# Six row products for four rows in the first convolution, the projection behind the gate, and input statistics on ScalarE

## The chip, the cores and the metric

The kernel runs on one core of a Trainium2 chip. The metric is the device time of one execution in microseconds (us). The three timed runs of the kernel before gave 3256.61, 3258.98 and 3260.0 us; their median is 3258.98 us.

## The reference, cut to what matters

The input `x` is float32 with shape 4 x 64 x 256 x 256. Two residual layers follow each other, each fed through a group norm (32 groups of two channels).

```python
# layer 0: x = x + L0(gn(x))
h = gelu(conv3x3(x, c1_w) + c1_b)               # 64 -> 64 channels
xa, k = split(c1x1(h, c2_w, c2_b))              # 64 -> 64 + 64
xs = gelu(depthwise 3x1 (depthwise 1x3 (xa)))
mask = top 2 of softmax(mean(xs over the image) @ gate_w.T)
out = xs + sum_i mask[i] * c1x1(c1x1(k, w2_i) * c1x1(xs, w1_i), w3_i)   # ranks 2, 4, 8
return c1x1(out, proj_w, proj_b)

# layer 1: x = x + L1(gn(x))
h = relu(batchnorm(conv3x3(x, quantized w1)))
h = batchnorm(conv3x3(h, quantized w2))
return relu(h + x)
```

The gate needs the mean of `xs` over a whole image, so the experts' share of an image can be added only after its last row has passed.

## The kernel before

Activations stand with 64 channels in each half of the 128 partitions, so that four matmuls of 64 x 64 can run side by side in the array. The work has four stages in time: statistics of image 0 and the weights; the *front* (layer 0, image after image, and within it what of layer 0's output can already be finished); *conv1* (the first convolution of layer 1, with the rest of layer 0's output between its steps); *conv2*; and the end, which adds and stores.

The front goes in steps of 8 rows ("octs", 128 of them). For the first convolution it uses a scheme that makes two neighbouring pixels of a row from four products: GpSimd forms the four combinations of the input (`front_v`, L493 to L501, eight additions of 128 x 256 per oct, into a ring `v_ring`), TensorE multiplies them with four sets of weights for each of three row taps (`front_conv_a`, `front_conv_b`, L547 to L562, all through the matmul of L458), ScalarE copies a part (L567), VectorE adds and subtracts in place (`front_butterfly`, L568 and L569), the other two products are added on top, and ScalarE applies the GELU (`front_h`, L575). The vertical taps are matmuls into bank `a` (`front_taps_a`, `front_taps_b`), the horizontal taps two VectorE operations (`front_taps_h`), then a GELU that also sums for the gate (`front_xs`, L645). `front_k` and `front_q` make the experts' 14 ranks for four octs at a time. `front_proj` (L665 to L696) multiplies `xs` with the projection, VectorE adds it to the resident input, and the sum goes to memory (`t1_d`). After the gate, `out_slot` (L770 to L798) loads that sum back, adds the experts with a 32-row matmul, and keeps statistics of the result.

The statistics of the next image's input are VectorE `bn_stats` (`stats_group`, L403). Between two halves of the vertical taps stands a small GpSimd memset, `divide` (L449 to L453), which waits for the first half and releases the second.

The order of the work is written out by hand: `at(step, order, call)` puts a call into a table, and the table is emitted in sorted order, so every engine runs its instructions in the order of those two numbers. In the front this holds for TensorE, SyncE's DMA queue, VectorE and GpSimd; ScalarE's order there was left to the scheduler. Each oct has its own tile of PSUM for the convolution:

```python
BANKS = {"c": 2, "a": 1, "p": 1}
return psum.tile([P, 2, GP, W], F32, tag=tag, name=name, bufs=BANKS[tag])
...
at(g, 1, front_conv_a, b, n, (1, 2))
at(place(g + 1), 3, front_conv_a, b, n, (0, 3))
at(g, 7, front_conv_b, b, n, (1, 2))
at(g, 7.5, front_butterfly, b, n)
```

Of the kernel before, what the change touches and what calls it, by code (L numbers as in the profile page):

```python
# [9 lines left out]
F32 = mybir.dt.float32  # L10
# [8 lines left out]
P = 128  # L19

NPAIR = H // 2
NSKEW = NPAIR + 1
PW = W + 2
GP = 2
# [14 lines left out]

@with_exitstack
def conv_preact_kernel(ctx: ExitStack, tc: tile.TileContext, io, col128, colset, col64):
    nc = tc.nc

    x_s = io["x"].rearrange("b c (two r) w -> b (c two) (r w)", two=2)
    out_v = io["out"].rearrange("b c (r two) w -> b two c r w", two=2)
# [8 lines left out]
    BANKS = {"c": 2, "a": 1, "p": 1}  # L77

    def bank(tag, name):
        return psum.tile([P, 2, GP, W], F32, tag=tag, name=name, bufs=BANKS[tag])  # L80
# [5 lines left out]


    t1_d = [dram.tile([P, NPAIR, W], F32, name=f"t1_d{b}") for b in range(B)]

    low_d = [dram.tile([P, NOCT // 4, 2 * GF], F32, name=f"low_d{b}") for b in range(B)]  # L90
    y_d = [dram.tile([P, NPAIR, W], F32, name=f"y_d{b}") for b in range(B)]
    y_v = [t.rearrange("(par c) (q half) w -> half par c q w", par=2, half=2) for t in y_d]
# [5 lines left out]

    RING = max(CPAIR * PW, (CPAIR + 1) * W)

    def place_in(name, fourth=False):
        return (spare if fourth else ring).tile([P, RING], F32, tag="in", name=name)

    def chunk_in(name, fourth):

        t = place_in(name, fourth)
        return t[:, 0 : CPAIR * PW].rearrange("p (a b) -> p a b", b=PW)

# [34 lines left out]

# [9 lines left out]

# [3 lines left out]

    VSLOTS = 12
    v_rings = [front_pool.tile([P, VSLOTS, 2, W // 2], F32, name=f"v_ring{i}") for i in range(2)]

    def v_of(p):

        return v_rings[p in (0, 3)][:, :, p // 2, :]

# [6 lines left out]

# [4 lines left out]
    ones = const.tile([P, P], F32, name="ones")  # L176
    nc.vector.memset(ones, 1.0)
# [13 lines left out]
    outer = lconst.tile([P, 2, W], F32, name="outer")  # L191
    wk = lconst.tile([P, 2, 2, 32], F32, name="wk")
# [7 lines left out]

    def weights():
# [3 lines left out]
        m64 = flat(m64_t)[0:C, 0 : io["m64"].shape[1]]  # L205
        nc.sync.dma_start(mset, io["mset"])
        nc.sync.dma_start(m64, io["m64"])
# [8 lines left out]

        nc.vector.tensor_tensor(flat(av), cset("c2_a"), cset("sv"), ALU.mult)


# [14 lines left out]


# [4 lines left out]
        for s in range(2):  # L240
            half = slice(s * C, s * C + C)
            for i in range(2):
                o = 16 * (i ^ s)
                nc.vector.tensor_copy(wk[half, s, i, o : o + NLOW], ps[half, 0:NLOW])
        nc.vector.memset(both, 0.0)
# [9 lines left out]

# [21 lines left out]

    def combine(mv, n, avg, eps_t, out, name):

# [26 lines left out]

# [71 lines left out]
    gn1, gn2, c1s, u12, v_edge, c1_bias = {}, {}, {}, {}, {}, {}  # L383
# [3 lines left out]

    st_x, x_in = {}, {}
# [15 lines left out]

    def stats_end(b):


        own = stat.tile([P, 2], F32, tag="gx", name=f"gx_{b}")
        yield from group_norm(st_x.pop(b), c128("avgx"), own, f"x{b}")
        yield  # L410
        gn1[b] = stat.tile([P, 2], F32, tag="gn1", name=f"gn1_{b}")
        v_edge[b] = lstat.tile([P, W // 2], F32, tag="v_edge", name=f"v_edge_{b}")
        ps = small(f"ps_gx_{b}")
        nc.tensor.matmul(ps[:, 0:2], c128("from_x"), own, start=True, stop=True)
        nc.vector.tensor_copy(gn1[b], ps[:, 0:2])
        c1s[b] = lstat.tile([P, 3, 3, C], F32, tag="c1s", name=f"c1s_{b}")

        engine = nc.gpsimd if b else nc.vector
        engine.tensor_scalar(
            c1s[b].rearrange("p a b c -> p (a b c)"), c128("c1"), gn1[b][:, 1:2], None, ALU.mult  # L420
        )
        engine.tensor_scalar(v_edge[b], zeros[:, 0 : W // 2], gn1[b][:, 0:1], 2.0, ALU.add, ALU.mult)
        u12[b] = lstat.tile([P, 3, 2, C], F32, tag="u12", name=f"u12_{b}")
        ends = lstat.tile([P, 3, C], F32, tag="u_ends", name=f"u_ends_{b}", bufs=1)
        engine.tensor_tensor(ends, c1s[b][:, :, 0, :], c1s[b][:, :, 2, :], ALU.add)
        for i, op in enumerate((ALU.add, ALU.subtract)):
            engine.tensor_tensor(u12[b][:, :, i, :], ends, c1s[b][:, :, 1, :], op)
        u = u12[b].rearrange("p a b c -> p (a b c)")
        engine.tensor_scalar(u, u, 0.5, None, ALU.mult)  # L429

        engine.tensor_tensor(ends[:, 0, :], u12[b][:, 0, 0, :], u12[b][:, 1, 0, :], ALU.add)
        for half in (slice(0, C), slice(C, P)):
            engine.tensor_tensor(both[half, half], ends[half, 0, :], u12[b][half, 2, 0, :], ALU.add)
        yield
        ps = small(f"ps_cb_{b}")
        nc.tensor.matmul(ps[:, 0:1], both, gn1[b][:, 0:1], start=True, stop=True)
        c1_bias[b] = stat.tile([P, 1], F32, tag="c1b", name=f"c1b_{b}")
        nc.vector.scalar_tensor_tensor(c1_bias[b], ps[:, 0:1], -2.0, c128("c1_b"), ALU.mult, ALU.add)


    xs_of, hs, xss, k_sb, pooled, open_c, open_a, open_t, open_p = {}, {}, {}, {}, {}, {}, {}, {}, {}


# [25 lines left out]
    def front_alloc(b, k):  # L469
        c = b * NCH + k  # L470
        if c % 5 == 3:
            xs_of[b, k] = chunk_x(f"x_{b}_{k}")
        else:
            xs_of[b, k] = chunk_in(f"x_{b}_{k}", c % 5 == 4)

    def front_load(b, k):

        x = xs_of[b, k]
        for half, slot, first in ((0, 0, 0), (0, 1, 1), (1, 0, 3), (1, 1, 2)):
            row = 2 * k * CPAIR + first  # L480
            nc.sync.dma_start(
                x[half * C : half * C + C, slot::2, 1 : 1 + W],
                io["x"][b][:, row : row + 4 * CG - 3 : 4, :],
            )

    def front_pad(b, k):
        edges = zeros[:, 0 : 2 * CPAIR].rearrange("p (a b) -> p a b", b=2)
        nc.gpsimd.tensor_scalar(xs_of[b, k][:, :, 0 : PW : PW - 1], edges, gn1[b][:, 0:1], None, ALU.add)

    def v_slot(b, n, slot):  # L490
        return (4 * (b * NOCT + n) + slot) % VSLOTS

    def front_v(b, n, half, products=((1, 2), (0, 3))):  # L493

        x = xs_of[b, n // 2]
        i = 4 * (n % 2) + 2 * half
        d = [x[:, i : i + 2, q : q + W - 1 : 2] for q in range(4)]
        terms = {0: (d[0], d[2], ALU.subtract), 1: (d[1], d[2], ALU.add), 2: (d[2], d[1], ALU.subtract), 3: (d[3], d[1], ALU.subtract)}
        o = v_slot(b, n, 2 * half)
        for p in (p for ps in products for p in ps):  # L500
            nc.gpsimd.tensor_tensor(v_of(p)[:, o : o + 2, :], *terms[p])  # L501

    def conv_tile(b, n, t, in_half, products, first, last):


        ps = open_c[b, n][:, t].rearrange("p a b -> p (a b)").rearrange("p (e q c) -> p e q c", e=2, q=GP)
        terms = {
            (0, 0): ([(1, 0), (2, 1)], [(0, 0), (1, 1)]),
            (0, 1): ([(0, -2)], [(2, 1)]),
            (1, 0): ([(0, 1)], [(2, 2)]),  # L510
            (1, 1): ([(1, 1), (2, 0)], [(0, 1), (1, 0)]),
        }[t, in_half]

        def pieces(slot, p):
# [822 lines left out]
```

## Time and profile before

| what | value |
|---|---|
| median of three runs | 3258.98 us |
| span of the profiled execution, first to last instruction | 3255.8 us |
| instructions | 61027 |
| TensorE (PE) busy | 2664.0 us, 82% |
| VectorE (DVE) busy | 2665.1 us, 82% |
| ScalarE (ACT) busy | 1647.6 us, 51% |
| GpSimd (POOL) busy | 1603.1 us, 49% |
| DMA moved | 832.01 MB, mean 256 GB/s |
| mean granted TensorE clock | 0.924 |

The runs' median is 3.2 us above the span of the profiled execution, whose own time outside its span the page does not give. The chain that ended last is 40% TensorE, 10% waits in SyncE's queue (in the end stage), 8% VectorE. A line of a group reads: source line, engine, operation, output <- input, shape, number of instructions, busy time and mean nanoseconds of one, then the idle time of the engine before them and what ended most of it. One float32 `matmul` of the program shows as two instructions. The clock is given as a share of full speed.

### The profile page before, as it was taken

The numbers are of one execution on the slowest core, as the hardware profiler recorded it, in microseconds if no ns is written. First come the engines' busy times: TensorE is split into PE (matmuls) and PEld (weight loads), VectorE is DVE, ScalarE is ACT, GpSimd is POOL, SyncE is SP. The second block draws the span as 40 slices with busy tenths as digits, with TensorE's granted clock in tenths as the row PEclk, the third lists the DMA queues.
The fourth block names the chain that finished last, engine by engine and source line by source line (L and its number), as shares of the span: only waits on it lengthen the run. The fifth ranks groups of instructions, "written<-read, shape, count | busy, mean of one in ns | idle before, by whom it ended". The sixth has DMA issues, their size and how long they took to land.

```text
span 3255.8 us, 61027 instructions
## 1 busy us (share of the span) xinstructions
PE 2664.0 (82%) x25080; PEld 1756.5 (54%) x25080; DVE 2665.1 (82%) x2810; ACT 1647.6 (51%) x1799; POOL 1603.1 (49%) x1833
## 2 busy tenths in 40 slices
PE   2999999999999999999999999989999999300000
PEld 1555555555555555555676677768787878200000
DVE  7676588878888777777899999979999999876655
ACT  0444443444434344446666666767777777432222
POOL 2444544444444534445687787757777777100000
PEclk9999999999999999999999999999999999655555
DMA  8665689879987777766788886656666663799999
GB/s 306 175 182 131 161 270 287 246 212 289 277 272 219 217 203 210 214 195 207 283 288 298 292 315 220 245 194 229 238 234 233 245 223 124 261 412 412 413 412 377
DMA packets 355591, 832.01 MB, mean 256 GB/s; under 512 B 22192, under 2 KB 284848, under 8 KB 293360
## 3 DMA queue, kind: packets, MB, share of 16 engines
q1 hardware_dynamic: 355312, 828.11, 76.5%
q8 instruction: 197, 3.23, 0.4%
q14 instruction: 82, 0.67, 0.1%
HBM read 489.85 MB, written 338.17 MB: 254 GB/s over the span
## 4 chain that ended last, share of the span: by engine, by line
PE 40%; SPq 10%; DVE 8%; DMA 3%; issue 3%; ACT 2%; POOL 1%; ACTq 0%; DVEq 0%; POOLq 0%
PE ps_h L316 22%; SPq L1224 7%; PE ps_c L458 5%; PE ps_h2m L316 4%; PE ps_a L458 3%; SPq L1219 2%; PE ps_hm L316 2%; DVE half L362 2%; DMA yn<-y_d 2%; DVE h L342 2%; PE ps_o L778 1%; PE ps_p L458 1%; SPq L1203 1%; DVE st_h L874 1%; DMA y_end<-y_d 1%
## 5 line engine op out<-in xcount | busy, mean ns | idle before, releaser
L316 PE MATMUL ps_h<-half,w_q 128*128 128x512 f32 x4096 | 1026.4, 402 | 20.4 <-DVE h L342 13.7
L316 PEld LDWEIGHTS ps_h<-half,w_q 128*128 128x128 f32 x4096 | 772.7, 190 | 249.4 <-DVE h L342 24.0
L381 POOL TENSOR_TENSOR sum<-s,sum 128x640 fp32r<-128x640 f32 (+1 forms) x256 | 557.2, 2197 | 199.4 <-ACT sum L379 193.8
L501 POOL TENSOR_TENSOR v_ring<-x 128x256 f32<-128x256 f32 x1024 | 591.2, 613 | 48.4 <-DMA x<-in_x 46.5
L458 PE MATMUL ps_c<-v_ring,u 64*64 64x256 f32 (+1 forms) x6472 | 389.1, 369 | 4.7 <-DVE u L429 3.5
L458 PE MATMUL ps_a<-h,av 64*64 64x512 f32 (+1 forms) x3568 | 383.5, 533 | 11.0 <-DVE t L628 8.6
L458 PE MATMUL ps_c<-v_ring,c1s 64*64 64x256 f32 (+1 forms) x6472 | 386.6, 370 | 5.0 <-POOL tick L451 4.5
L342 DVE SCALAR_TENSOR_TENSOR h<-ps_h,scale_w,m 128x1024 f32<-128x1024 f32 x256 | 326.7, 1276 | 73.0 <-ACT m L341 72.9
L575 ACT ACTIVATE h<-ps_c,c1b 128x512 f32<-128x512 f32 x256 | 174.1, 742 | 403.5 <-PE ps_c L458 403.5
L458 PEld LDWEIGHTS ps_c<-v_ring,c1s 64*64 64x64 f32 x6472 | 250.5, 133 | 202.3 <-issue 72.2
L458 PEld LDWEIGHTS ps_c<-v_ring,u 64*64 64x64 f32 x6472 | 270.4, 133 | 144.0 <-POOL v_ring L501 66.0
L451 POOL MEMSET tick<- 128x1 f32 x132 | 13.0, 98 | 679.2 <-PE ps_a L458 668.5
L645 ACT ACTIVATE xs<-t 128x1024 f32<-128x1024 f32 x128 | 135.4, 1058 | 368.9 <-DVE t L631 351.4
L1215 ACT ACTIVATE v<-y_end,shift,gn 128x2048 f32<-128x2048 f32 x64 | 133.8, 2092 | 293.8 <-DMA y_end<-y_d 260.9
L362 DVE TENSOR_TENSOR half<-h,half 128x1280 fp32r<-128x1280 f32 (+1 forms) x128 | 254.3, 2028 | 7.7 <-ACT half L360 7.7
L1216 DVE SCALAR_TENSOR_TENSOR h<-h,ss,v 128x2048 f32<-128x2048 f32 x64 | 149.9, 2349 | 134.5 <-ACT v L1215 84.4
L690 DVE TENSOR_TENSOR x<-ps_p,x 128x1024 f32<-128x1024 f32 x128 | 156.1, 1219 | 101.1 <-PE ps_p L458 69.0
L568 DVE TENSOR_TENSOR ps_c<-m,ps_c 128x512 f32<-128x512 f32 x128 | 89.0, 695 | 175.8 <-ACT m L567 175.7
L458 PEld LDWEIGHTS ps_a<-h,av 64*64 64x64 f32 x3568 | 163.5, 133 | 128.5 <-issue 91.7
L362 DVE TENSOR_TENSOR half<-yn,half 128x1280 fp32r<-128x1280 f32 x80 | 202.7, 2551 | 0.0
L341 ACT ACTIVATE m<-ps_hm,m,scale_w 128x512 f32<-128x512 f32 x128 | 99.4, 777 | 183.2 <-PE ps_hm L316 153.9
L786 DVE SCALAR_TENSOR_TENSOR y<-ps_o,ob,y 128x1024 f32<-128x1024 f32 x128 | 163.6, 1278 | 15.1 <-PE ps_o L778 10.9
(186 smaller groups left out, 4083.5 us busy)
## 6 DMA issues: line engine op xcount, KB each, us to landing
h_d<-h SPq DMA_DIRECT2D x114, 1024.0 KB, 4.8
h<-h_d SPq DMA_DIRECT2D x64, 1152.0 KB, 7.1
yn<-y_d SPq DMA_DIRECT2D x60, 1152.0 KB, 8.3
xs_in<-in_x SPq DMA_DIRECT2D x64, 1024.0 KB, 9.0
x<-in_x SPq DMA_DIRECT2D x256, 256.0 KB, 5.3
y<-t_d SPq DMA_DIRECT2D x64, 1024.0 KB, 8.8
y_d<-y SPq DMA_DIRECT2D x256, 256.0 KB, 5.1
y_end<-y_d SPq DMA_DIRECT2D x64, 1024.0 KB, 10.8
```

The costliest lines, as they stand in the source:

```text
L316: nc.tensor.matmul(ps[:, 0 : n * HW], w[:, k, m, :], t[:, i + m : i + m + n, c : c + HW], start=(j == 0), stop=(j == len(terms) - 1),)
L342: nc.vector.scalar_tensor_tensor(h.rearrange("p a (b e) -> p e (a b)", e=2), by_two(ps)[:, :, 0 : n * HW], w_scale[w], m.unsqueeze(1).to_b ...
L362: engine.tensor_tensor(lower, y, upper.bitcast(F32), ALU.subtract)
L381: nc.gpsimd.tensor_tensor(tiles[1][:, a:e, :], t, tiles[0][:, a:e, :].bitcast(F32), ALU.subtract)
L458: last[:] = [nc.tensor.matmul(ps[o, at_out[0] : at_out[1], :], w[i], rhs[i], **flags)]
L501: nc.gpsimd.tensor_tensor(v_of(p)[:, o : o + 2, :], *terms[p])
L575: nc.scalar.activation(h.rearrange("p q (c e) -> p e q c", e=2), c[:, t].rearrange("p (e q c) -> p e q c", e=2, q=GP), AF.Gelu, bias=c1_bi ...
L645: nc.scalar.activation(flat(xss[b, n]), flat(open_t.pop((b, n))), AF.Gelu, accum_out=pooled[b][:, n : n + 1])
L690: nc.vector.tensor_tensor(t1, ps, t1, ALU.add)
L786: nc.vector.scalar_tensor_tensor(y, ps.rearrange("p i a b -> p (i a) b"), out_bias[b], y, ALU.add, ALU.add)
L1216: nc.vector.scalar_tensor_tensor(h, h, ss2[:, 0:1], v, ALU.mult, ALU.add)
L1224: nc.sync.dma_start(chunk_h2(b2, k2), h2_d[b2][:, k2 * CPAIR : (k2 + 1) * CPAIR, :])
```

## The change

The first convolution is now done in *units* of 16 rows (64 of them), eight rows in each half of the partitions with their neighbouring rows loaded too. Four rows of output are made from six products instead of two pixels from four, with three column taps each. GpSimd makes the six combinations from twelve additions of 128 x 512 (`x_differences`, `v_inner`, `v_outer`), ScalarE makes scaled copies (`x_four`, `x_scaled`), and one tile `v` holds them. TensorE runs three calls of 24 matmuls per unit: products 1 and 2, products 3 and 4, and products 0 and 5, which are added on top after the butterflies. The convolution's PSUM is one tile `c4` of four banks that every unit uses again; slots 0 and 1 of a half share a bank, slots 2 and 3 the next. VectorE's butterflies are eight operations of 128 x 512 per unit.

`front_proj` and the sum in memory are gone. `xs` itself goes to memory (`xs_d`), and `out_open` multiplies it with the projection after the gate, together with the experts (rearranged to 64 rows); `out_load` reads the input once more. `out_slot` has three parts, so that its matmuls, addition and statistics can stand at different places. The statistics of images 1 to 3 are ScalarE `Identity` and `Square` passes with accumulators. The weights of the six products are made on GpSimd at the start. ScalarE's order in the front is now written out as well. In the order table, a slot `u` has places 0 to 6 in its first step and 6 to 12 in its second. Layer 1 is not changed, but ten output parts of image 2 instead of four now fall into conv1's time.

```diff
-    BANKS = {"c": 2, "a": 1, "p": 1}
+    c4 = psum.tile([P, 2, 2 * GP, W], F32, name="c4")
+    c_turn = count()
     def bank(tag, name):
-        return psum.tile([P, 2, GP, W], F32, tag=tag, name=name, bufs=BANKS[tag])
+        if tag == "c":
+            return c4[:, next(c_turn) % 2].rearrange("p (t q) w -> p t q w", t=2)
+        return psum.tile([P, 2, GP, W], F32, tag=tag, name=name, bufs=1)
...
+    def stats_piece(b, n):
+        t = x_in[b, n // 2][:, n % 2 * 2 * GP : (n % 2 + 1) * 2 * GP, :]
+        t = t.rearrange("p a b -> p (a b)")
+        for i, f in enumerate((AF.Identity, AF.Square)):
+            bias = shift_x[b] if i == 0 else 0.0
+            nc.scalar.activation(t, t, f, bias=bias, accum_out=st_x[b][:, i, n : n + 1])
...
+    def x_four(u):
+        x4s[u] = front_pool.tile([P, 2, 2, W], F32, tag="x4", name=f"x4_{u}")
+        inner = xt[u][:, 1:9, :].rearrange("p (g r) w -> p r g w", r=4)[:, 0:2]
+        nc.scalar.activation(x4s[u], inner, AF.Copy, scale=4.0)
+    def x_differences(u):
+        x, x4 = xt[u], x4s[u]
+        for j in (1, 2):
+            nc.gpsimd.tensor_tensor(x4[:, j - 1], x_rows(u, j + 2), x4[:, j - 1], ALU.subtract)
+        x_edges(u)
+        for r in range(0, 8, 2):
+            nc.gpsimd.tensor_tensor(x[:, r : r + 2], x[:, r + 2 : r + 4], x[:, r : r + 2], ALU.subtract)
...
+    def front_conv(u, products):
+        slot = {1: 0, 2: 1, 3: 2, 4: 3, 0: 2, 5: 3}
+        calls = [(i, kx) for i in products for kx in range(3)]
+        opens = products != (0, 5)
+        rounds(*([((c4[:, h], o, h, us[b][:, i, kx, :], v[:, i, o : o + 1, kx : kx + W], (slot[i], slot[i] + 1)),
+                   dict(start=(opens and n == 0), stop=(n == len(calls) - 1), skip_group_check=True),)
+                  for n, (i, kx) in enumerate(calls)] for h in range(2) for o in range(2)))
+    def front_copy(u, n):
+        nc.scalar.activation(mcs[u][:, n], c4[:, :, 2 * n, :], AF.Copy)
+    def butterfly_a(u):
+        m = mcs[u][:, 0]
+        nc.vector.tensor_tensor(c4[:, :, 0, :], m, c4[:, :, 1, :], ALU.subtract)
+        nc.vector.tensor_tensor(c4[:, :, 1, :], m, c4[:, :, 1, :], ALU.add)
+    def butterfly_b(u):
+        nc.vector.tensor_tensor(d2, m, c4[:, :, 3, :], ALU.subtract)
+        nc.vector.tensor_tensor(m, m, c4[:, :, 3, :], ALU.add)
+    def butterfly_c(u):
+        nc.vector.tensor_tensor(c4[:, :, 2, :], mcs[u][:, 1], c4[:, :, 1, :], ALU.add)
+        nc.vector.scalar_tensor_tensor(c4[:, :, 3, :], d2s[u], 8.0, c4[:, :, 0, :], ALU.mult, ALU.add)
+    def butterfly_d(u):
+        nc.vector.scalar_tensor_tensor(c4[:, :, 1, :], s2, 4.0, c4[:, :, 1, :], ALU.mult, ALU.add)
+        nc.vector.scalar_tensor_tensor(c4[:, :, 0, :], d2, 2.0, c4[:, :, 0, :], ALU.mult, ALU.add)
+    def front_h(u, inner):
+        ps = c4[:, :, 0:2, :] if inner else c4[:, :, 2:4, :]
+        nc.scalar.activation(hs[u][:, :, rows, :], ps, AF.Gelu, bias=c1_bias[u // NCH])
...
+    def out_open(b, n):
+        rounds(*([((ps[:, x], p, x, c128("proj"), xs[:, :, p, :], (0, 2)), ...),
+                  ((ps[:, x], p, x, wm[b][:, i, :], low[:, :, p, :], (0, 2)), ...)]
+                 for x in range(2) for p in range(2)))
...
+    def plan_front():
+            if 2 <= u + 2 <= last:
+                at_slot(u, 0, x_load, u + 2)
+                at_slot(u, 1, front_conv, u, (1, 2))
+                at_slot(u, 1.1, front_copy, u, 0)
+                at_slot(u, 1.3, front_conv, u, (3, 4))
+                at_slot(u, 1.35, butterfly_a, u)
+                at_slot(u, 1.4, front_copy, u, 1)
+                at_slot(u, 2.1, butterfly_b, u)
+                at_slot(u, 4.05, butterfly_c, u)
+                at_slot(u, 4.1, butterfly_d, u)
+                at_slot(u, 4.2, front_h, u, True)
+                at_slot(u, 5, front_conv, u, (0, 5))
+                at_slot(u, 5.1, front_h, u, False)
+                at_slot(u, 0.5, x_differences, u + 1)
+                at_slot(u, 1.5, x_scaled, u + 1)
+                at_slot(u, 2.3, v_inner, u + 1)
+                at_slot(u, 5.5, v_outer, u + 1)
+                at_slot(u, 7.1, x_four, u + 2)
+                at_slot(u, 2, front_taps_a, u - 2, 1)
+                at_slot(u, 2.2, divide)
+                at_slot(u, 4, front_taps_b, u - 2, 1)
+                at_slot(u, 4.15, front_taps_i, u - 2, 1)
+                at_slot(u, 5.2, front_taps_h, u - 2, 1)
+                at_slot(u, 5.3, front_xs, u - 2, 1)
+                at_slot(u, 7, front_taps_a, u - 1, 0)
+                at_slot(u, 7.2, divide)
+                at_slot(u, 9, front_taps_b, u - 1, 0)
+                at_slot(u, 9.1, front_taps_i, u - 1, 0)
+                at_slot(u + 1, 1.15, front_taps_h, u - 1, 0)
+                at_slot(u + 1, 1.2, front_xs, u - 1, 0)
+            if u % 2 == 0:      # four octs at a time
+                    at_slot(u, 3, front_q, *divmod(j, NOCT // 4))
+                    at_slot(u, 4, front_low, *divmod(j, NOCT // 4))
+                    at_slot(u, 8, front_k, *divmod(j, NOCT // 4))
+    def plan_out(b, count):
+        t = NCH * (b + 1) + 4
+        for n in range(count):
+            u, i = t + 2 * (n // 4), n % 4
+            u, pos = ((u, 6), (u + 1, 3), (u + 1, 6), (u + 1, 8))[i]
+            at_slot(u, pos, out_open, b, n)
+            add, st = {6: (6.1, 6.2), 3: (4.12, 6.05), 8: (8.1, 8.2)}[pos]
+            at_slot(u, add, out_add, b, n)
+            at_slot(u, st, out_stats, b, n)
```

## The prediction, on record before the result

> **What bounds the kernel now.** I read the page's engine table and its slices first, then the busy times by stage, TensorE's order of time, one of its pauses, and the groups by shape.
>
> ```profile
> PE 2664.0 (82%) x25080; PEld 1756.5 (54%) x25080; DVE 2665.1 (82%) x2810; ACT 1647.6 (51%) x1799; POOL 1603.1 (49%) x1833
> ...
> PE   2999999999999999999999999989999999300000
> ```
>
> The 82% is an average: before the end stage every slice of TensorE is at 9 tenths, bar the first and three others. By stage (columns PE, PEld, DVE, ACT, POOL) the front is TensorE's; in conv1 VectorE is nearly level with it, and ScalarE has much room in the front.
>
> ```profile
> 480.00:880.00 400.00, 394.36 (x5510) 215.25 (x5506) 343.78 (x447) 164.74 (x233) 179.84 (x351) 1.00 0.87 260
> 1520.00:2180.00 660.00, 635.04 (x2627) 473.56 (x2625) 614.58 (x601) 435.08 (x428) 489.27 (x290) 0.99 0.78 271
> ```
>
> TensorE's order of time gives the pace: first convolution matmul, the gates of images 0 and 1, first conv1 matmul. The front lasts 1465.5 - 66.2 = 1399 us; 16 rows take 356.5/16 = 22.3 us between gates, and in image 0, whose gate falls 35.3 octs after its start, 20.2 us.
>
> ```profile
> 66.24 3.29 PE L458 MATMUL ps_c<-v_ring,u 64*64 64x256 f32 x32 [3.46 <-DVE u L429]
> ...
> 423.65 0.39 PE L721 MATMUL ps_g<-m,spread 128*128 128x9 f32 x2
> ...
> 780.11 0.39 PE L721 MATMUL ps_g<-m,spread 128*128 128x9 f32 x2
> ...
> 1465.53 4.02 PE L316 MATMUL ps_h<-half,w_q 128*128 128x512 f32 x16
> ```
>
> Inside an oct the matmul groups follow each other without a gap; the distance of the starts is the price.
>
> ```profile
> 809.15 1.96 PE L458 MATMUL ps_c<-v_ring,u 64*64 64x256 f32 x32
> 811.04 1.13 PE L778 MATMUL ps_o<-ranks,wm 32*128 32x512 f32 x4
> 812.10 1.96 PE L458 MATMUL ps_c<-v_ring,c1s 64*64 64x256 f32 x32
> 813.88 1.90 PE L458 MATMUL ps_a<-h,av 64*64 64x512 f32 x20
> ```
>
> And one place shows what a pause does: after 2.49 us of idling, eight projection matmuls take 1.98 instead of 1.03 us. In the 4 us from 1451 on the granted clock is 0.57 (last columns: clock, DMA share, GB/s), and 1.6 us are lost until it is whole.
>
> ```profile
> 1451.51 1.98 PE L458 MATMUL ps_p<-xs,m 64*64 64x512 f32 x8 [2.49 <-DVE y L786]
> 1453.25 1.83 PE L458 MATMUL ps_c<-v_ring,c1s 64*64 64x256 f32 x20
> ```
>
> ```profile
> 1451.00:1455.00 4.00, 3.49 (x32) 2.36 (x36) 2.88 (x4) 0.00 (x0) 0.00 (x0) 0.57 0.57 134
> ```
>
> The prices on the other engines, from the groups by shape:
>
> ```profile
> L645 ACT ACTIVATE xs<-t 128x1024 f32<-128x1024 f32 x128 | 135.4, 1058 | 368.9 <-DVE t L631 351.4 <-DVE t L640 17.5
> L567 ACT ACTIVATE m<-ps_c 128x512 f32<-128x512 f32 x128 | 76.8, 600 | 9.0 <-PE ps_c L458 9.0
> L569 DVE TENSOR_TENSOR ps_c<-m,ps_c 128x512 f32<-128x512 f32 x128 | 89.0, 696 | 4.4
> L381 POOL TENSOR_TENSOR sum<-s,sum 128x512 fp32r<-128x512 f32 x128 | 261.1, 2040 | 0.0
> L367 POOL TENSOR_TENSOR s<-yn 128x512 f32<-128x512 f32 x64 | 66.6, 1040 | 0.0
> ```
>
> **The change as work.** TensorE: 32 convolution instructions run in 1.78 us (812.10 to 813.88), so a call of 24 matmuls (48 instructions) takes 2.67, and 2.85 to its last result (a group's 1.96 is 0.18 longer than its pace). Three calls are 8.0 us per unit against 2 x (1.89 + 1.78 + 0.88 + 0.86) = 10.8 for two octs before: 2.8 x 64 = 179 us less. The projection moves at its price, and the experts' four matmuls of 64 rows (0.86, as the projection) replace two of 32 rows (1.06). VectorE loses the projection's addition (156 us) and 192 of 256 input statistics (130 us), and gains four butterflies per unit (4 x 0.70 x 64 = 178 us). ScalarE gains 192 statistics passes at 1.06 + 0.19 us for the accumulator (240 us) and 2.8 us of scaled copies per unit. GpSimd does twelve additions of 512 at 1.04 us instead of sixteen of 256 at 0.61: 12.5 instead of 9.8 us per 16 rows. No engine's sum exceeds 19 us per unit, so on sums alone this wins.
>
> **The change as a chain.** The waits of the changed kernel, as built, say otherwise. All accesses to `c4` are put in one line, though the slots differ: products 3 and 4 wait for ScalarE's copy of products 1 and 2; the first butterfly waits for the last matmul of products 3 and 4; the second copy waits for that butterfly; products 0 and 5 wait for the inner GELU, which stands behind the last butterfly; the next unit's products 1 and 2 wait for the outer GELU. Reason: an access to one slot of both halves spans the other slots of the first half. Before, each oct had its own tile, and an oct's second pair ran while the next oct's first pair stood open.
>
> One slot from the start of products 1 and 2, with 0.05 to 0.1 us per hand-over (VectorE's `ps_c` ended at 73.00, TensorE began at 73.06): products 1, 2 to 2.85; copy 2.95 to 3.55; products 3, 4 to 6.45; butterfly a 6.55 to 7.95; second copy 8.0 to 8.6; butterfly b to 10.1. TensorE meanwhile has taps (1.75 before, as 813.88 to the next group; now 1280 columns per quarter of the array instead of 1024, 2.2), then `front_q` or `out_open` (1.85), then taps (0.5): idle from 11.0 on, with the next output, the other taps and `front_k` queued behind products 0, 5.
> - Odd slots: VectorE is through c and d at 12.9, but ScalarE has in its queue after the second copy two scaled copies (1.75), a pair of statistics passes (2.4) and the taps' copy (1.21, L624's mean) before the GELU (1.21, same row): 15.15. Products 0, 5 start at 15.2.
> - Even slots: `front_low` (1.28, as L706) stands on VectorE before butterfly c and waits for `front_q` until 10.5; c and d end at 14.6, the GELU at 15.9; start at 16.0.
>
> These pauses of 4.2 and 5.0 us are longer than the 2.49 us above, so products 0, 5 start on the lower clock: 2.85 + 1.6 = 4.45. Then `out_open` 1.75, taps 2.2, `front_k` or another `out_open` 1.9, taps 0.5, in all 6.35. Slot: 26.0 odd, 26.8 even, mean 26.4 against 22.3.
> Image 0 (slots 2 to 19) has no `out_open`, but ScalarE, still at the previous slot's statistics, makes the first copy 0.65 (odd) to 1.15 us (even) late: products 0, 5 end at 15.8 + 4.45 = 20.3 and at 21.6; with taps 2.2, 0.3 for `divide`, taps 0.5 the odd slot is 23.3, with `front_k` the even one 26.2, mean 24.8. Without statistics (slots 47 to 63) the odd GELU goes at 12.9: 25.0 and 26.8, mean 25.9. Slots 0 and 1 are the bare chain, 20 us each.
> Sum of the front: 2 x 20 + 18 x 24.8 + 27 x 26.4 + 17 x 25.9 = 1640 us, 241 more. In the start, GpSimd's queue as built has a little operation that waits for the group norm (63.0 us) ahead of unit 0's differences; eight operations later, at 71, products 1, 2 can start: +5.
> Conv1 has 42 output parts at 1.75 instead of 36 at 1.06, 35 us; the fewer `front_proj` in the overlap give back 4. TensorE is 96% busy there, so I take 30, bounds 0 and 35. Conv2 and the end have the same code.
> Sum: 3255.8 + 241 + 5 + 30 = 3532, and 3.2 for the distance of the median: **3535 us**.
>
> Prices that the trace does not show. GpSimd's 512-element addition lies between 1.04 (L367) and 2.04 (L381, rounded output); types are L367's, so 1.04; 2.04 makes twelve 24.5 us, still under a slot, but the 2x copy a microsecond later: +64. `Square` lies between 1.06 (L645) and 1.21 (L624); I take 1.06; the built kernel has 20 table loads like the old one. The lower clock per pause costs 0 to 1.7 us: 62 x 1.6 = 99 us downwards. DMA: stored and reloaded `xs` replaces the stored sum; one more reading of x and the neighbouring rows add 84 MB, 7 MB per slot or 265 GB/s, under the 289 of the window 870 to 970. On SyncE's queue a store of `xs` waits for its GELU and holds later loads up; the next needed load has 12 us, a similar one landed in 8.8 (median). If that cover went, `out_open` would wait.
>
> The Trainium skill ("PSUM — Partial Sum Buffer", section "PSUM bank collisions raise a hardware error") wants PSUM guarded by bank and quadrant. By it the copy and butterflies of one bank could run beside products in another; the sum would be the first rival's. I go by the waits built in. The skill's "TensorE: Matmul & The Clock Gate" (section "What's actually happening") lets the clock fall after an idle window of about 3.4 us; the row shows 2.49 suffices. By the page, image 3's odd pauses (3.3 us) would be free: 13 us less.
>
> **The rivals.**
> - *The chain is covered, and the products' saving shows* (faster). Were c4's slots waited for singly, products 0, 5 would wait only for butterfly c: nothing in odd slots, 2.4 us in even ones. TensorE's own sum is 8.0 + taps 5.4 + two outputs 3.5 + k and q 1.9 = 18.8, with the even wait 20.0; in image 0 ScalarE's 17.6 and that wait, 18.8. Front 2 x 20 + 18 x 18.8 + 44 x 20.0 = 1258: 3259 - 141 + 5 + 30 = 3153. For it: every sum under 19 us. Against: the built waits. It decides when slots average below 21.3 us.
> - *The chain stands, but the clock stays up*: 3535 - 99 = 3436. For it: TensorE works two thirds of each slot. Against: 1451.51.
> - *Slower still*: GpSimd's differences at L381's price, 64 us, and TensorE's wait for the first copy, 0.8 to 2 us, also costing clock in image 0, 18 x 1.6 = 29: 3628.
>
> **How the numbers follow.** Chances: forecast 0.60 (own range 3470 to 3600), clock stays up 0.20, slower still 0.11, covered 0.07, unchanged 0.02. The range 3400 to 3630 takes in the first three with conv1's bound. 0.2% is about what a measurement of this kernel can tell from no change: faster 0.07, same 0.02, slower 0.91.
>
> **What would show it.** Right: gates 420 us apart (images 1, 2) instead of 356; the largest idle of TensorE before products 0, 5, released by ScalarE's GELU, 3 to 5 us long, 64 times; a granted clock well below 1 in the front; VectorE waiting for TensorE in the first butterfly. Wrong: TensorE at 95% in the front, or the largest waits at GpSimd's `v` or at a DMA; the step that fails is then the chain, or the price of the additions.

## The result

The changed kernel takes 4352.8 us (median of 4, 4348.07 to 4362.67) against 3258.3 of the kernel before on the same chip: 1.336 times as long, 95% interval 1.3339 to 1.3381. The forecast was 3535, with a range of 3400 to 3630. The direction was right; the size was a quarter of the 1094 us that came. The profiled execution took 4348.1 us, its span is 4346.3.

The page of the kernel after, engine table and two rows of its slices:

```profile
PE 2760.2 (64%) x22112; PEld 1681.7 (39%) x22112; DVE 2650.3 (61%) x2764; ACT 1998.4 (46%) x2250; POOL 1965.0 (45%) x1514
...
PE   1666667777777777677777777766676676750000
...
PEclk9888888888888888889999999999999999985555
```

TensorE was at 9 tenths in nearly every slice; now it is at 6 or 7, and not only in the front: the low digits go on to the end stage. The busy times by stage say it in numbers (columns: PE, PEld, DVE, ACT, POOL, granted clock, DMA share, GB/s). Here are a part of the front, conv1 alone and conv2 of the kernel after,

```profile
480.00:880.00 400.00, 292.11 (x3716) 144.04 (x3712) 235.81 (x294) 228.53 (x320) 226.10 (x208) 0.86 0.75 217
2200.00:2800.00 600.00, 448.92 (x1899) 309.48 (x1900) 393.34 (x362) 269.54 (x266) 307.58 (x179) 0.95 0.61 203
2940.00:3880.00 940.00, 661.97 (x2521) 492.44 (x2522) 571.01 (x507) 446.48 (x436) 431.41 (x257) 0.95 0.38 136
```

and conv2 of the kernel before:

```profile
2200.00:2790.00 590.00, 587.37 (x2499) 469.41 (x2499) 563.76 (x503) 445.76 (x435) 429.38 (x255) 1.00 0.60 217
```

Conv2 runs the same matmuls (some 2,500 instructions), but in 940 us instead of 590. TensorE's order of time gives the stages of the changed kernel, by the same marks as before (first convolution matmul, gates of images 0 and 1, first conv1 matmul):

```profile
78.37 1.98 PE L457 MATMUL c<-v,us 64*64 64x256 f32 x16 [9.88 <-POOL v L519]
...
581.61 0.39 PE L708 MATMUL ps_g<-m,spread 128*128 128x9 f32 x2
...
1025.05 0.39 PE L708 MATMUL ps_g<-m,spread 128*128 128x9 f32 x2
...
1853.04 4.02 PE L291 MATMUL c<-half,w_q 128*128 128x512 f32 x16
```

With the first and the last write of `ps_h2m` as marks for conv2, the difference falls apart so (us):

| stage | before | forecast | after |
|---|---|---|---|
| start, to the first convolution matmul | 66.2 | 71 | 78.4 |
| front, to the first conv1 matmul | 1399 | 1640 | 1775 |
| conv1 | 728 | 758 | 1082 |
| conv2 | 600 | 600 | 949 |
| from there to the end of the span | 462 | 462 | 463 |

So 703 of the 1094 us are lost in conv1 and conv2, where the forecast had 30. Among the groups by shape (busy, mean ns | idle before it, releaser) TensorE's largest idle time stands at L291, the matmuls of these two convolutions; the front's L457 comes second, and ScalarE's L662 waits for `front_q`, which the forecast had not seen:

```profile
L291 PE MATMUL c<-half,w_q 128*128 128x512 f32 x4128 | 1136.2, 431 | 547.2 <-DVE h L317 539.6
L457 PE MATMUL c<-v,us 64*64 64x256 f32 x9216 | 679.3, 451 | 453.6 <-ACT h L594 383.3
...
L662 ACT ACTIVATE xs<-t 128x1024 f32<-128x1024 f32 x128 | 134.7, 1052 | 290.8 <-PE ps_q L688 221.1
```

One part of conv2 after (16 matmul instructions into one half of `c4`, and what reads them), in order of time:

```profile
3506.78 4.01 PE L291 MATMUL c<-half,w_q 128*128 128x512 f32 x16 [2.19 <-DVE h L317]
3510.64 1.09 PE L291 MATMUL ps_h2m<-sum,w_q 128*128 128x512 f32 x4
3511.76 0.78 ACT L316 ACTIVATE m<-ps_h2m,m,scale_w 128x512 f32<-128x512 f32 x1 [4.15 <-PE ps_h2m L291]
...
3512.57 1.28 DVE L317 SCALAR_TENSOR_TENSOR h<-c,scale_w,m 128x1024 f32<-128x1024 f32 x1 [4.52 <-ACT m L316]
...
3513.91 4.01 PE L291 MATMUL c<-half,w_q 128*128 128x512 f32 x16 [2.19 <-DVE h L317]
```

and before:

```profile
2506.74 3.94 PE L316 MATMUL ps_h<-half,w_q 128*128 128x512 f32 x16
...
2509.98 1.27 DVE L342 SCALAR_TENSOR_TENSOR h<-ps_h,scale_w,m 128x1024 f32<-128x1024 f32 x1
...
2511.46 3.91 PE L316 MATMUL ps_h<-half,w_q 128*128 128x512 f32 x16
```

Before, the part at 2506.74 runs while VectorE still reads the part ahead of it (2509.98): two buffers. After, matmuls, ScalarE's `m`, VectorE's `h` and the next matmuls stand in one row: 3.86 + 1.09 + 0.78 + 1.28 and the hand-overs make the 7.13 us from 3506.78 to 3513.91. So the matmuls that write one half of `c4` wait for VectorE's L317, which reads the other half: `bank("c")` takes the halves in turn.

### The profile page after: what moved, and what is told of

Read it like the earlier page. It is cut to its first block, busy times and chain, and to the rows that moved or that the text cites. A ratio compares the mean times of both kernels' runs of the same rounds, so it can differ in the third digit from the quotient of the medians.

```text
span 4346.3 us, 54988 instructions
## 1 busy us (share of the span) xinstructions
PE 2760.2 (64%) x22112; PEld 1681.7 (39%) x22112; DVE 2650.3 (61%) x2764; ACT 1998.4 (46%) x2250; POOL 1965.0 (45%) x1514
## 4 chain that ended last, share of the span: by engine, by line
PE 30%; DVE 11%; SPq 7%; ACT 5%; issue 2%; DMA 1%; POOL 0%; DVEq 0%; ACTq 0%
PE c L291 24%; DVE h L317 7%; SPq L1276 4%; ACT m L316 4%; PE ps_h2m L291 3%; PE ps_hm L291 2%; SPq L1271 2%; DVE half L337 1%; SPq L1255 1%; PE ps_o L457 1%; DVE h L1268 1%; DVE st_h L886 0%; DVE y L796 0%; DMA out<-h 0%; DMA y<-in_x 0%
## 5 line engine op out<-in xcount | busy, mean ns | idle before, releaser
L291 PE MATMUL c<-half,w_q 128*128 128x512 f32 x4128 | 1136.2, 431 | 547.2 <-DVE h L317 539.6
L291 PEld LDWEIGHTS c<-half,w_q 128*128 128x128 f32 x4128 | 821.3, 205 | 876.5 <-DVE h L317 657.3
L457 PE MATMUL c<-v,us 64*64 64x256 f32 x9216 | 679.3, 451 | 453.6 <-ACT h L594 383.3
L317 DVE SCALAR_TENSOR_TENSOR h<-c,scale_w,m 128x1024 f32<-128x1024 f32 x256 | 328.7, 1284 | 689.1 <-ACT m L316 689.0
L457 PEld LDWEIGHTS c<-v,us 64*64 64x64 f32 x9216 | 402.5, 160 | 707.3 <-ACT h L594 387.3
L457 PE MATMUL ps_a<-h,av 64*64 64x512 f32 x4080 | 388.5, 496 | 24.0 <-DVE t L643 13.4
L505 POOL TENSOR_TENSOR x<-x 128x512 f32<-128x512 f32 x256 | 326.8, 1277 | 15.5
L640 DVE SCALAR_TENSOR_TENSOR t<-ps_a,m,t 128x1020 f32<-128x1020 f32 x128 | 163.0, 1274 | 271.6 <-ACT t L634 271.6
L594 ACT ACTIVATE h<-c,c1b 128x1024 f32<-128x1024 f32 x128 | 142.4, 1112 | 368.3 <-PE c L457 317.2
L662 ACT ACTIVATE xs<-t 128x1024 f32<-128x1024 f32 x128 | 134.7, 1052 | 290.8 <-PE ps_q L688 221.1
L457 PEld LDWEIGHTS ps_a<-h,av 64*64 64x64 f32 x4080 | 147.7, 135 | 294.1 <-issue 263.3
L533 POOL TENSOR_TENSOR v<-x 128x512 f32<-128x512 f32 x64 | 81.9, 1280 | 333.0 <-PE c L457 333.0
L342 POOL TENSOR_TENSOR s<-h 128x640 f32<-128x640 f32 (+1 forms) x128 | 145.7, 1159 | 121.0 <-ACT h L1147 120.7
```

Of the source, the lines that this page charges most:

```text
L291: nc.tensor.matmul(ps[:, 0 : n * HW], w[:, k, m, :], t[:, i + m : i + m + n, c : c + HW], start=(j == 0), stop=(j == len(terms) - 1),)
L317: nc.vector.scalar_tensor_tensor(h.rearrange("p a (b e) -> p e (a b)", e=2), by_two(ps)[:, :, 0 : n * HW], w_scale[w], m.unsqueeze(1).to_b ...
L342: nc.gpsimd.tensor_tensor(t, y[:, a:e, 0::2], y[:, a:e, 1::2], ALU.add)
L457: last[:] = [nc.tensor.matmul(ps[o, at_out[0] : at_out[1], :], w[i], rhs[i], **flags)]
L505: nc.gpsimd.tensor_tensor(x[:, r : r + 2], x[:, r + 2 : r + 4], x[:, r : r + 2], ALU.subtract)
L640: nc.vector.scalar_tensor_tensor(t[:, :, 1:W], ps[:, :, 0 : W - 1], sh[:, 0:1], t[:, :, 1:W], ALU.mult, ALU.add)
```

## The experiments

The theory after this result: the kernel as built treats the two halves of `c4` as overlapping, so `bank("c")` no longer gives two buffers. That costs conv1 and conv2 their overlap, and makes the front's chain. Rivals: the convolutions are slow for another reason (memory, clock, `m`); the front's chain comes from the order of the queues.

**e1 and e2: the two convolutions.** e1 is the changed kernel, with two tiles for conv1 and conv2 only:

```diff
+    c4 = c_front.enter_context(tc.tile_pool(name="c_front", bufs=1, space=PSUM)).tile(...)   # front
 def bank(tag, name):
     if tag == "c":
-        return c4[:, next(c_turn) % 2].rearrange("p (t q) w -> p t q w", t=2)
+        return c_conv[0].tile([P, 2, GP, W], F32, tag="c", name=name, bufs=2)
 def conv1_open():
     front.close()
+    c_front.close()
+    c_conv.append(ctx.enter_context(tc.tile_pool(name="c_conv", bufs=2, space=PSUM)))
```

e2 is the reverse: the kernel before, whose conv1 and conv2 take the two halves of one tile by the changed kernel's line.

> The changed kernel with its front left as it is (six products on the one tile c4), and two separate tiles in turn for the sums of Layer 1's two convolutions. Theory (the two halves of c4 count as overlapping, so that conv1 and conv2 have lost their double buffer): conv1 and conv2 together go back from 2034 us to about 1331 + 35, the front stays at 1775, total 4352 - 670 = about 3680 (3640 to 3720); TensorE's 2.19 us wait for VectorE's `h` before each part of conv2 is gone. Rival (the convolutions are slowed by something that the one tile does not cause: memory traffic, the granted clock, ScalarE's copy `m`): they stay near 2000 us and the total is above 4200.

> The kernel before, all of it, but for conv1 and conv2, whose sums become the two halves of one tile, as in the changed kernel. Theory (the one tile by itself takes the double buffer from both convolutions): conv1 and conv2 take about 2000 instead of 1331 us, total 3259 + 650 to 700 = about 3930; TensorE waits 2 us for VectorE's `h` before each part of conv2. Rival (it is the rest of the change, or the convolutions' place behind the new front): total 3260 +- 20.

Measured: e1 3717.5 us (1.140 of before, 1.1376 to 1.1422), 635 less than the changed kernel; e2 3929.6 (1.205, 1.2025 to 1.2073), 668 more than the kernel before. TensorE's waits for `h` over the whole span (us in total, times, longest), for before, after, e1 and e2 in turn:

```profile
PE ps_h L316 <- DVE h L342: 13.7, 12, 4.0
```

```profile
PE c L291 <- DVE h L317: 539.6, 253, 6.4
```

```profile
PE ps_h L292 <- DVE h L318: 11.2, 10, 2.1
```

```profile
PE c L323 <- DVE h L349: 537.1, 253, 4.8
```

The wait goes and comes with the one tile alone, in a kernel that has nothing else of the change. Conv2 takes 599.5 us in e1 and 949 in e2. The theory holds for both convolutions, and the rival falls. Conv1 in e1 takes 799 us, 71 more than before: that part has another cause (below).

**e3: two tiles by pair of slots.** Slots 0 and 1 of both halves in one tile, 2 and 3 in another; `bank("c")` takes them in turn:

```diff
-    c4 = psum.tile([P, 2, 2 * GP, W], F32, name="c4")
+    cs = [psum.tile([P, 2, GP, W], F32, name=f"c4_{i}") for i in range(2)]
-            return c4[:, next(c_turn) % 2].rearrange(...)
+            return cs[next(c_turn) % 2]
-   (c4[:, h], o, h, ..., (slot[i], slot[i] + 1))
+   (cs[slot[i] // 2][:, h], o, h, ..., (slot[i] % 2, slot[i] % 2 + 1))
```

> The changed kernel with c4 cut into two tiles by pair of slots (slots 0 and 1 of both halves; slots 2 and 3), in the front as in the convolutions. Theory (one tile costs twice: the chain in the front, and the double buffer of the convolutions): convolutions as in e1; in the front products 3 and 4 no longer wait for the first copy, nor the next products 1 and 2 for the outer GELU; slots fall from 27.5 us to between TensorE's own 20 and 24 (what is left is the wait of products 0 and 5 for butterfly c and, in even slots, ScalarE's wait of about 4 us for a buffer of xs), front 1260 to 1500, total 1907 + front = 3170 to 3410. Rival (the order of the queues, not the tile, makes the front's chain): front stays near 1775, total as e1, about 3680.

Measured: 3509.7 us (1.077, 1.0751 to 1.0789). The front falls from 1777 (e1) to 1559: the single tile also made the front's chain, so the rival falls. But 1559 lies above the 1260 to 1500 expected. What is left, in an even slot of e3 (ScalarE's `xs`, then the second copy, then TensorE's products 0 and 5):

```profile
646.65 1.06 ACT L662 ACTIVATE xs<-t 128x1024 f32<-128x1024 f32 x1 [6.00 <-PE ps_q L688]
...
647.71 0.58 ACT L562 ACTIVATE mc<-c 128x512 f32<-128x512 f32 x1
...
652.31 5.37 PE L457 MATMUL c<-v,us 64*64 64x256 f32 x48 [5.13 <-DVE c L580]
```

**e4 and e5: `front_q` earlier.** The same edit to the changed kernel (e4) and to e3 (e5):

```diff
-   at_slot(u, 3, front_q, *divmod(j, NOCT // 4))
-   at_slot(u, 4, front_low, *divmod(j, NOCT // 4))
+   at_slot(u, 0.95, front_q, *divmod(j, NOCT // 4))
+   at_slot(u, 1.02, front_low, *divmod(j, NOCT // 4))
```

> The changed kernel, c4 one tile as it is, with `front_q` and `front_low` moved from the middle of the even slot to its start (places 0.95 and 1.02, ahead of products 1 and 2). In the even slots of the changed kernel ScalarE's `xs` waits 6.9 us for `front_q`, since one of the four buffers of `xs` comes free only then, and holds the second copy behind it. Theory (that wait lies on the front's chain of even slots): the even slots lose 4 to 5 us of their pause and keep the clock no better than before, 31 slots: 4352 - 120 to 200, about 4190. Rival (the wait is covered by the chain on c4, the GELU comes no earlier): 4352 +- 20. Conv1 and conv2 as in the changed kernel in both.

> The two tiles of e3 and the early `front_q` of e4 together. In e3's even slots TensorE idles 5.1 us before products 0 and 5 and then runs them in 5.4 instead of 2.8 us, because the second copy stands on ScalarE behind the `xs` that waits for `front_q`. Theory (this is what is left of the front's chain): the pause and the lower clock go, up to 7 us in each of some 31 even slots, front 1559 - 160 to 220, total 3290 to 3350. Rival (another wait takes its place: VectorE's or ScalarE's queue is as late for another reason): total stays above 3430.

Measured: e4 4309.1 us (1.322, 1.3193 to 1.3246), 44 less; e5 3466.6 (1.064, 1.0619 to 1.0655), 43 less than e3. Both gains are well below what the theory expected. In e4 the even slot's products 0 and 5 come 14.7 us after products 1 and 2, as in odd slots, instead of 18.64: the wait was on the chain.

```profile
693.36 2.82 PE L457 MATMUL c<-v,us 64*64 64x256 f32 x48
696.90 2.82 PE L457 MATMUL c<-v,us 64*64 64x256 f32 x48 [0.72 <-ACT mc L562]
...
708.05 4.61 PE L457 MATMUL c<-v,us 64*64 64x256 f32 x48 [5.27 <-ACT h L594]
...
788.67 5.26 PE L457 MATMUL c<-v,us 64*64 64x256 f32 x48 [4.03 <-ACT h L594]
```

But the gain comes in images 0 and 3 (33 and 13 us up to their gates); in images 1 and 2 nearly all of it is given back. `front_q` had filled TensorE's pause for nothing, and at the slot's start it costs its 1.9 us and a wait of 1 us for `y`; and in odd slots (788.67) products 0 and 5 take 5.3 us after the same pause after which they took 4.1. Gates 0 and 1 are 443.4 us apart in both kernels. In e5 new waits come out in images 1 and 2 (window 600 to 1500):

```profile
PE ps_k L672 <- DVE y L796: 66.5, 13, 7.9
DVE y L796 <- DMA y<-in_x: 51.7, 10, 8.8
```

TensorE waits for VectorE's output addition, which waits for its load. By stage, image 0 (no output yet) and image 1 of e5:

```profile
200.00:470.00 270.00, 223.21 (x2956) 112.86 (x2948) 164.41 (x206) 200.34 (x283) 195.26 (x181) 0.92 0.58 176
600.00:860.00 260.00, 209.47 (x2732) 100.59 (x2736) 181.11 (x232) 160.17 (x221) 159.31 (x147) 0.93 0.98 282
```

In image 1 the DMA engines are busy 0.98 of the time. Slots are 21.4 us in image 0 (by the distances of `ps_k`) and 24.6 in image 1 (by the gates). Is it the bytes, or the order of the one queue?

**e6 and e7: bytes, or order.** e6 takes 47 MB of reading out of e5, e7 only reorders:

```diff
 # e6, plan_stats and stats_piece
-   at_slot(max(int(slots[k] - 2), 0), 0.1, stats_load, b, k, "s", 4)
+   if k == 0: at_slot(max(int(slots[k] - 2), 0), 0.1, stats_load, b, k, "s", 4)
-   t = x_in[b, n // 2][...]
+   t = x_in[b, 0][...]
 # e7, plan_out
-   at_slot(u, 0.4, out_load, b, k)
+   at_slot(u - 1, 6.3, out_load, b, k)
-   at_slot(u, 5.6, out_load, b, k + 1)
+   at_slot(u, 0.4, out_load, b, k + 1)
```

> e5, but of x for the statistics of images 1 to 3 only one chunk per image is read from memory and used for all passes, so the statistics are not those of the image; ScalarE's passes are all still there. This takes some 47 MB of reading out of the front, 1.05 of about 6.75 MB per slot. Theory A (in images 1 and 2 of e5 the front waits for memory: the engines of the DMA are busy 0.94 to 0.98 at 270 to 282 GB/s, and 6.75 MB at 275 GB/s are the 24.8 us of a slot): slots fall from 24.8 to the 21.4 of image 0, some 30 slots, total 3466 - 70 to 110, about 3375. Rival B (not the bytes but SyncE's queue, in which the loads of `y` stand behind stores that wait for ScalarE): gain below 30, total 3440 to 3470.

> e5 with the loads of x for the residual (`y`, `out_load`) put earlier in SyncE's queue: each first one from (u, 0.4) to (u - 1, 6.3), each second one from (u, 5.6) to (u, 0.4). The bytes are the same. Theory A (memory is the limit): VectorE's wait for `y` (52 us in the window 600 to 1500 of e5) only moves to another load; gain below 30, total 3440 to 3470. Rival B (the order in SyncE's queue): the waits of VectorE's `y` for a DMA go, and TensorE's 67 us before `ps_k` behind them, total 3370 to 3410.

Measured: e6 3421.2 us (1.049, 1.0476 to 1.0507), 45 less than e5, between the two theories. (With the bytes e6 takes the loads themselves out of SyncE's queue; what is called "the bytes" here and below is both together.) e7 3517.4 (1.080, 1.0778 to 1.0824), 51 more, outside both. In e7 VectorE no longer waits for `y`; SyncE's queue does, and holds up what stands behind (window 600 to 1500):

```profile
SPq L750 <- DMA y_d<-y: 171.0, 36, 6.5
```

The early load waits for its buffer (two for `y`, each filled again only when its store is through), and the loads of x behind it come late: ScalarE waits 57 us for x, which is not among its larger waits in e5. The edit was put before the buffer was free, so it settles nothing about the order.

**e8 and e9: the stores of `xs` from ScalarE.**

```diff
-   nc.sync.dma_start(xs_d[b][:, n, :], flat(x))
+   nc.scalar.dma_start(xs_d[b][:, n, :], flat(x))
-   at_slot(u, 5.6, out_load, b, k + 1)
+   at_slot(u, 3.5, out_load, b, k + 1)
```

> e5 with the stores of `xs` issued by ScalarE, right behind the GELU that makes them, instead of SyncE (in e5 SyncE's queue waits 270 us of the window 600 to 1500 in these stores for that GELU, with loads queued behind), and each second load of `y` at (u, 3.5) instead of (u, 5.6). The bytes are the same. If the order of SyncE's queue costs what is left in images 1 and 2 (B): VectorE's waits for `y` and TensorE's before `ps_k` (67 us in that window) go, total 3466 - 60 to 110, about 3385. If it is the memory (A): the loads land later instead, total 3440 to 3470; as in e7, a wait for another load appears.

> e8 and e6 together (the stores of `xs` from ScalarE, and the statistics of images 1 to 3 from one chunk each, so not those of the image). If both the order and the bytes cost, each hidden by the other in e6 and e7: slots of images 1 and 2 near the 21.4 us of image 0, total 3320 to 3350. If the order alone: as e8. If the bytes alone: as e6, 3420.

Measured: e8 3506.2 us (1.076, 1.0743 to 1.078), 40 more than e5; e9 3456.9 (1.061, 1.0584 to 1.0628), 49 less than e8. Both miss. The bytes are worth 45 to 49 us with either queue. In e8 VectorE's wait for `y` grew from 52 to 99 us in the same window. e8 makes two edits at once, so it does not say which of them costs; why the loads came later is open. SyncE's queue waits 223 us there for VectorE's additions before the stores of `y`, against 69 in e5, but that may be a consequence.

**e10: the statistics back on VectorE**, in e5:

```diff
-   for i in range(2): ... at_slot(int(s), 1.6 or 7.15, stats_piece, b, 2 * k + i)
+   for i in range(4):
+       s = slots[k] + i * per / 4
+       at_slot(int(s), 7.15 if s - int(s) < 0.5 else 8.3, stats_group, b, CG * k + i)
```

> e5 with the statistics of x of images 1 to 3 back on VectorE, four passes per slot at (u, 7.15) and (u, 8.3), as the kernel before has them; the part of the change that put them on ScalarE is undone. Theory C (ScalarE's queue is what is left of the chain in the slots with statistics: its two pairs of passes, 4.8 us per slot, stand ahead of the taps' copy, which VectorE's `t` waits for): slots 2 to 46 lose 1 to 2 us, image 0 comes from 21.4 to near 20 us, total 3466 - 40 to 90, about 3400. Rival (the passes fill time in which ScalarE has nothing to do, and VectorE gets 2.7 us more per slot): total 3466 to 3500.

Measured: 3418.8 us (1.049, 1.0476 to 1.0511), 48 less than e5, nearly all of it in image 0: its gate comes at 431.3 instead of 475.0, while gates 0 and 1 are 399.6 apart against 393.1. The part of the change that put the statistics on ScalarE costs 48 us here; in images 1 and 2 something else sets the pace. In image 0 the new scheme now does what it was made for: two slots take 36.6 us (`ps_k` comes once in two slots),

```profile
206.57 1.95 PE L672 MATMUL ps_k<-h,wk 64*32 64x512 f32 x32
...
243.13 1.95 PE L672 MATMUL ps_k<-h,wk 64*32 64x512 f32 x32
```

18.3 each. From the first convolution matmul to gate 0 it is only 4.5 us less than before (352.9 against 357.4): slots 0 and 1 and the last ones of the image take longer than 18.3.

**e11 and e12: the first load of `y` alone, and less to read.** e11 is e10 with one place changed, e12 reads one chunk per image for the statistics, as e6:

```diff
-   at_slot(u, 0.4, out_load, b, k)
+   at_slot(u - 1, 8.9, out_load, b, k)
```

> e10 with the first load of `y` of each pair of slots issued at (u - 1, 8.9) instead of (u, 0.4), that is ahead of the loads of x for the next units and the statistics instead of behind them, but, other than in e7, late enough that its buffer is free and SyncE's queue is not held up. In e10 TensorE waits 70 us of the window 600 to 1500 before `ps_k` for VectorE's `y`, which waits for that load. If the order of the loads is what sets images 1 and 2: slots 25.0 to about 23, total 3419 - 40 to 70, about 3365. If the bytes are (engines of the DMA busy 0.90 to 0.96 there): the load of x or another comes later, total 3405 to 3450.

> e11, but of x for the statistics of images 1 to 3 only one chunk per image is read and used for all groups, so the statistics are not those of the image; the passes stay. 47 MB less to read. If the bytes set images 1 and 2: total 60 to 100 below e11. If nothing of the memory is left once the order is right: within 20 of e11.

Measured: e11 3369.0 us (1.033, 1.0312 to 1.0346), 50 less than e10 as the order's theory has it; e12 3320.5 (1.020, 1.0165 to 1.0234), 49 less than e11, where the bytes alone were expected to give 60 to 100 and the order alone under 20. So both count, some 50 us each. The bytes' own sign came in e11 too: ScalarE now waits 51 us for loads of x in the window 600 to 1500, against 2 in e10. In e11 the window of image 1 moves more than in e5:

```profile
600.00:860.00 260.00, 213.87 (x2798) 107.53 (x2794) 218.27 (x295) 121.16 (x148) 163.56 (x152) 0.94 0.95 294
```

e11 is the fastest version of the changed kernel that computes everything, and still 3.3% slower than the kernel before: no faster one was found. Of the 113 us between the two spans, 68 lie in conv1, 33 in the front and 12 in the start.

## Why the prediction was wrong

Its sum was 3535. Four terms were off, and together they close it, with e1 for the split: the lost buffer of conv1 and conv2, 635 (4352.8 - 3717.5); the front, 135; conv1's outputs, 41; the start, 7: 3535 + 818 = 4353.

- **The step that failed**: "Conv2 and the end have the same code", which put conv2 at nothing, and conv1's 30 us; 349 and 354 us came. The lines are the same, but the tile behind the name `c` had changed, and I had read the built waits of the front only. My reason for them, that an access to one slot of both halves "spans the other slots of the first half", was too narrow: e1 and e2 show that an access to one half alone already waits for the other. The end did stay (463 us).
- **The chain in the front**: the mechanism was right, its size in even slots was not. One odd and one even slot of the kernel after (products 1 and 2, products 0 and 5, then the next slot; ScalarE's `xs` and second copy):

```profile
642.26 2.77 PE L457 MATMUL c<-v,us 64*64 64x256 f32 x48
...
656.90 4.14 PE L457 MATMUL c<-v,us 64*64 64x256 f32 x48 [4.02 <-ACT h L594]
...
666.88 2.76 PE L457 MATMUL c<-v,us 64*64 64x256 f32 x48
...
677.26 1.06 ACT L662 ACTIVATE xs<-t 128x1024 f32<-128x1024 f32 x1 [6.94 <-PE ps_q L688]
...
678.32 0.58 ACT L562 ACTIVATE mc<-c 128x512 f32<-128x512 f32 x1
...
685.52 5.18 PE L457 MATMUL c<-v,us 64*64 64x256 f32 x48 [7.73 <-ACT h L594]
...
696.86 2.77 PE L457 MATMUL c<-v,us 64*64 64x256 f32 x48
```

  The odd slot: products 0 and 5 at 14.64 (forecast 15.2), 24.6 in all (26.0). The even slot: at 18.64 (16.0), 30.0 in all (26.8). I had counted `front_q` as TensorE's work and `front_low` as VectorE's, but not the four buffers of `xs` that `front_q` frees: ScalarE's `xs` waits 6.94 us, and the second copy stands behind it. e4 takes that wait away and the even slot's products come at 14.7. In image 0 e4 brings gate 0 from 581.6 to 549.0; the forecast's terms put it at 71 + 2 x 20 + 16.6 x 24.8 = 523. The marks named for the chain came: TensorE waits for ScalarE's GELU 65 times, 383 us in all, VectorE for TensorE before the first butterfly 51 times.
- **The clock**: right. A pause of 4.02 us makes 4.14 of 2.8, one of 7.73 makes 5.18; the forecast took 4.45 for both. (After 4.03 us it was 5.26 in e4: the loss is not fixed by the pause.) The granted clock was 0.86 in the window shown. The rival "the clock stays up" falls.
- **Slower still**: its mechanisms did not come. GpSimd's additions of 512 took 1.28 us instead of 1.04, 2.9 us per slot more, but GpSimd waits for TensorE (333 us before L533). TensorE's wait for the first copy was between 0.7 and 3.7 us in image 0 and mostly 0.73 later, which the main forecast held in part. The range reached up to this rival, which saw only the front; even without the convolutions' loss, e1's 3717 would lie outside it.
- **Covered and faster**: e3, e5, e10 and e11 are its test, each with one more wait taken away. The front went 1777, 1559, 1521, 1479, 1432 us, never near 1258, and not below the 1399 of before. In image 0 of e10 the slots of 18.3 us are near this rival's 18.8, though with the statistics on VectorE, not for its reason. From image 1 on the engine sums of under 19 us leave out the memory: the forecast had checked its 7 MB per slot at 26.4 us, 265 GB/s, but in 18.8 us they would need 372, where image 1 of e11 moved 294. The whole kernel moves 915.0 MB instead of 832.0; e12, with 47 MB of them gone, comes to 1380.
- **Start and conv1**: the first matmul came 12 us later, not 5. Conv1's outputs: in e1 the `ps_o` matmuls keep TensorE busy for 88 us of conv1 against 41 before, 48 more instead of the 35 forecast. TensorE is also idle 24 us longer there, 11 of them before `ps_o` matmuls that wait for reloaded `xs`; together that makes the 71.
- **The two rules**: by the Trainium skill's "PSUM — Partial Sum Buffer" (section "PSUM bank collisions raise a hardware error") guarding by bank and quadrant would do. The kernel as built guards `c4` as one piece, and that decides its time; e3, with the same work on two tiles, shows the difference: 4352.8 against 3509.7. No run here guards by bank and quadrant. Of "TensorE: Matmul & The Clock Gate" (section "What's actually happening"), the idle window of about 3.4 us agrees with the pauses of odd slots in images 1 to 3, which were 3.5 to 4.0 us and cost the clock; image 3's were 3.52 us, not the 3.3 of the forecast. It does not agree with the pause of 2.02 us below.

## What to carry to other kernels

When a change turns buffers of a pool into views of one tile, look up in the built waits every user of that name, the loops whose code did not change too: two halves are two buffers only if the kernel's builder keeps them apart. Of each instruction that is late, list what it frees as well as what it computes; a buffer freed late stops another engine's queue. And before engine sums are taken as the new pace, divide the bytes of a slot by what memory gave in that stage.

## What was not expected of the hardware

A pause of about 2 us had two outcomes in one and the same loop. In e5's front the same 24 matmul instructions of the taps follow the same pause of 2.02 us in two slots of the same kind (`ps_k` comes next in both), and take 4.05 us in one and 2.38 in the other:

```profile
218.68 4.05 PE L457 MATMUL ps_a<-h,av 64*64 64x512 f32 x24 [2.02 <-DVE t L643]
...
263.32 2.38 PE L457 MATMUL ps_a<-h,av 64*64 64x512 f32 x24 [2.02 <-DVE t L643]
```

The granted clock is 0.57 in the 4 us after the first pause and 1.00 after the second, with the DMA engines about equally busy (0.56 and 0.53):

```profile
218.70:222.70 4.00, 4.00 (x29) 1.32 (x31) 0.07 (x1) 3.82 (x6) 1.27 (x2) 0.57 0.56 172
263.30:267.30 4.00, 3.98 (x56) 1.44 (x56) 0.11 (x1) 3.78 (x6) 2.73 (x5) 1.00 0.53 169
```

Conv2 of the kernel after shows the same with matmuls that use the whole array. A pause of 2.19 us stands before nearly every part; most parts then take 4.0 us, as at 3506.78 above, but 22 of some 125 take 5.4 to 5.6, mostly one in six, 44.4 us apart:

```profile
3498.12 5.56 PE L291 MATMUL c<-half,w_q 128*128 128x512 f32 x16 [2.19 <-DVE h L317]
...
3542.45 5.55 PE L291 MATMUL c<-half,w_q 128*128 128x512 f32 x16 [2.19 <-DVE h L317]
```

So neither the length of the pause nor the matmuls behind it decide alone. What does is open. The forecast's "2.49 suffices" is one outcome of such a pause, not a rule.

The DMA engines were busy 0.98 at 282 GB/s in image 1 of e5 and 0.95 at 294 in e11, where the end stage of the kernel after moved 412: a busy share near 1 is no fixed number of bytes.
